# A spectral network with fused head and dilation: PSUM as single and triple tiles, and a new order of bursts, sums and head steps

## The chip, the cores and the metric

The kernel runs on one core of a Trainium2 chip. The metric is device time in microseconds (us), the median of repeated runs of the whole program. The engines are TensorE (PE in the profile; PEld is its weight load), VectorE (DVE), ScalarE (ACT), GpSimd (POOL) and SyncE (SP, which here only starts transfers). TensorE writes its results to PSUM, an on-chip memory of eight banks; a bank has 512 float32 columns on 128 partitions. VectorE and ScalarE read the banks and write to SBUF, the large on-chip memory. All arithmetic is float32, and one float32 matmul appears in the trace as two instructions ("x32" for 16 matmuls).

## The reference

The input is 8 images of 8 channels and 256 x 256 pixels. Channels fall into 4 groups.

```python
def net(x):                                   # x: group-normalised image
    h = conv1x1(concat(x, gridx, gridy))      # fc0, 4 groups x 10 channels
    for i in range(4):
        f = rfft2(h)                          # only 24 x 12 coefficients are used
        f = einsum('bgixy,gioxy->bgoxy', f, w[i])
        h = irfft2(f) + conv1x1(h, w_w[i], w_b[i])
        if i < 3: h = swish(h, beta[i])
    h = swish(conv1x1(h, fc1), beta[3])       # 4 groups x 128 hidden
    return conv1x1(h, fc2)                    # 2 channels a group

x = x + net(group_norm(x))
x = x + dilation3x3(group_norm(x))            # maximum of 9 shifted copies
```

## The kernel before

**Stages of an image.** The spectra are truncated, so each transform is a small matrix product. `spectrum_x` (L231) normalises the image and forms the first layer's spectrum; `spectrum_h` (L326) does so for layers 1 to 3 from rows that were summed while the layer before ran. `mix` (L361) multiplies the spectrum with the weights on VectorE, and TensorE folds the result. `rows_of` (L406) turns it into `zt`, the coefficients of every row, in five rounds of two outputs each, with one two-bank PSUM tile a round (matmuls L413, or L417 in odd layers; copies L195). Then `layer` (L432) goes over the image in 11 chunks, taken in 6 pairs (the last pair has one chunk).

**What a layer does with a chunk.** The four pieces are functions within `layer`.

- `burst(c)` fills four banks: 16 matmuls for the 1x1 convolution (L488; L485 in layer 0), then 8 that add the inverse transform from `zt` (L491). ScalarE empties the banks with two activations (SiLU at L497; in layer 3 an addition of a bias at L499, and the chunk is stored to DRAM).
- `turn(c)`: VectorE transposes the chunk in 32 x 32 blocks, in two halves (L439), into one of three parts of the buffer `turned`.
- `transform(k)` is the row transform of pair k, which the next layer's spectrum needs: 32 matmuls into four banks (L456), and two copies of 960 columns back into `turned` (L201 on VectorE, L199 on ScalarE).
- `gather(k)` sums the result over the blocks with a constant matrix (4 matmuls into one bank, L470), and VectorE copies it into `zt` (L473, or L476 for pairs whose chunks lie the other way round).

**The head of the image before.** Between these pieces run the 128 steps of the previous image's fc1 and fc2. `first(n)` is fc1 for 512 pixels a group: 4 matmuls into four banks (L635) and two SiLU activations of 1024 columns (L637). `second(n)` is fc2 for two steps together: 8 matmuls into one bank (L657), which VectorE adds to the residual (L662; L660 for the first of each eight). A step n that is even does `second(n - 4)` and then `first(n)`; an odd one does only `first(n)`. So an even step has 12 matmuls, an odd one 4.

**Who sets the order.** The order on TensorE, VectorE and ScalarE is the program's. A layer is a generator; each `yield (1,)` in it runs one head step and after it one operation of the dilation of an earlier image (`dilate`, L686 to L722: maxima at L704, L706, L709 with L710, and a normalising and adding part to L720). The strings "even" and "odd" make one extra step if the count of steps has the other parity, so that the even steps fall where the layer wants them. Numbers that are yielded outside the layers (spectrum, mix, rows) are shares of a step; there the head fills the gaps. Layers 0 to 2 take 11 steps each, layer 3 takes two for each chunk. Image 0 has no head beside it, and the last image's head runs alone at the end.

```python
        for k in range((NCH + 1) // 2):
            c = 2 * k
            burst(c)
            if k > 1: gather(k - 2)
            yield (1,)          # even head step: second, first
            turn(c)
            burst(c + 1)
            if k > 0: transform(k - 1)
            yield (1,)          # odd head step: first
            turn(c + 1)
```

**PSUM.** All tiles have one tag, "z": two banks each, four buffers, used in turn. A burst, a transform and a first take two of these tiles, a rows_of round takes one, and everything that needs one bank (`ps_a`: gather, second, the sums of the normalisation) takes a whole tile of two and uses half of it. A tile is reused as soon as its reader has finished, so with four buffers a group of four banks can be filled while the group before it is emptied.

Of the kernel before, what the change touches and what calls it, by code (L numbers as in the profile page):

```python
# [19 lines left out]
HW = 256  # L20
# [24 lines left out]
def fno_dilate_kernel(ctx: ExitStack, tc: tile.TileContext, a: dict, out: bass.AP):  # L45
# [10 lines left out]
    def ps_z(name):  # L56
        return ps.tile([128, 2, 512], F32, tag="z", bufs=4, name=name)

    def ps_a(name):
        return ps_z(name)[:, 0, :]  # L60
# [91 lines left out]
    p = ps_z("p_wc")  # L152
# [43 lines left out]

    def copy_2(i, dst, src):
        if i % 2:
            nc.scalar.activation(dst, src, AF.Identity)  # L199
        else:  # L200
            nc.vector.tensor_copy(dst, src)  # L201

# [28 lines left out]
    def spectrum_x(b, out_):  # L231
# [22 lines left out]
        for half in range(2):  # L254
            xn = x[:, half].rearrange("p (r w) -> p r w", r=8)
            for r in range(0, 8, 4):
                t = ps_z(f"p_xt_{b}_{half}_{r}")
                for i in range(8):
                    nc.tensor.transpose(
                        t[:, i // 4, 128 * (i % 4) : 128 * (i % 4 + 1)],  # L260
                        xn[:, r + i // 2, 128 * (i % 2) : 128 * (i % 2 + 1)], ident,
                    )
                dst = xt[half][:, :, r : r + 4, :].rearrange("p f (u r) c -> p u r f c", u=2)
                src = t.rearrange("p u (r f c) -> p u r f c", r=2, f=2)
                for u in range(2):
                    copy(u, dst[:, u], src[:, u])
                yield 1.4
# [138 lines left out]
    def rows_of(b, l):  # L406

        zv = zt[:, :, :, : NBLK * WID].rearrange("p r f (n o) -> p o n r f", n=NBLK)
        for o in range(0, WID, 2):
            p = ps_z(f"p_g_{b}_{l}_{o}")  # L410
            for u in range(2):
                if l % 2 == 0:
                    mm(p[:, u, : NBLK * CS * NQ], fz[:, o + u].rearrange("p g k -> p (g k)"),  # L413
                       rowg.rearrange("p n j r -> p (n j r)"), start=True, stop=True)
                else:
                    for g in range(G):
                        for j in range(NQ):  # L417
                            mm(p[part(j), u, NBLK * CS * g : NBLK * CS * (g + 1)], fz[:, o + u, g, :],
                               rowg[:, :, j, :], start=True, stop=True)
            for u in range(2):  # L420
                src = p[:, u, : NBLK * CS * NQ]
                if l % 2 == 0:
                    dst = zv[:, o + u].rearrange("p n r f -> p n f r")
                    src = src.rearrange("p (n f r) -> p n f r", n=NBLK, r=CS)
                else:
                    dst = zv[:, o + u].rearrange("p n r f -> p f n r")
                    src = src.rearrange("p (f n r) -> p f n r", f=NQ, n=NBLK)
                copy(u, dst, src)
            yield 0.7


    def layer(b, l, out_, stored, side):  # L432
        group_in_f = l % 2 == 1

        def turn(c):

            dst = turned[:, c % 3].rearrange("p (s f x) -> p f s x", s=2, f=NQ)
            for i in range(2):
                nc.vector.transpose(  # L439
                    dst[:, 2 * i : 2 * i + 2], h[:, c, 2 * i : 2 * i + 2].rearrange("p f (s x) -> p f s x", s=2))  # L440
# [5 lines left out]
        def transform(k):  # L446
# [6 lines left out]
            pair = [ps_z(f"p_d_{b}_{l}_{k}_{i}") for i in range(2)]  # L453
            for v in range(8):
                for q in range(NQ):
                    mm(pair[q // 2][part(v % 4), q % 2, : 240 * n], fw8[part(q), v, :],  # L456
                       t[part(q), :, :, v, : NBLK * WID], start=v < 4, stop=v >= 4)
            e = turned[:, (2 * k + 1) % 3, : 960 * n].rearrange("p (q x) -> p q x", q=NQ)
            for i in range(2):
                copy_2(i, e[:, 2 * i : 2 * i + 2], pair[i][:, :, : 240 * n])  # L460

        def gather(k):
# [5 lines left out]
            for g in range(NQ):  # L468
                m = e[:, :, :, g] if group_in_f else e[:, g].rearrange("p q r i -> p r q i")
# [8 lines left out]
        def burst(c):  # L478
            pair = [ps_z(f"p_z_{b}_{l}_{c}_{i}") for i in range(2)]
            for f in range(NQ):  # L480
                for q in range(NQ):
                    o = pair[q // 2][part(f), q % 2, :]
# [6 lines left out]
            for s in range(2):  # L489
                for q in range(NQ):  # L490
                    mm(pair[q // 2][:, q % 2, HW * s : HW * (s + 1)],  # L491
                       zt[part(q), 2 * c + s].rearrange("p f o -> p (f o)"), binv[part(q), :],
                       start=False, stop=s == 1)
            for i in range(2):
                dst = h[:, c, 2 * i : 2 * i + 2, :]
                if l < 3:
                    nc.scalar.activation(dst, pair[i], AF.Silu)  # L497
                else:
                    nc.scalar.activation(dst, pair[i], AF.Identity, bias=bias3)  # L499
# [8 lines left out]
        if l == 0:  # L508
# [3 lines left out]
            nc.vector.tensor_scalar(wcn, wc, out_["mr"][:, 1:2], None, ALU.mult)  # L512
        if l == 3:

            yield "odd"
# [6 lines left out]
        yield "even"  # L522
        for k in range((NCH + 1) // 2):
# [5 lines left out]
            turn(c)  # L529
            if c + 1 < NCH:  # L530
                burst(c + 1)
            if k > 0:
                transform(k - 1)
# [81 lines left out]
    def head(b, stored, stats):  # L615
# [13 lines left out]
        def first(n):  # L629
# [3 lines left out]
            pair = [ps_z(f"p_fc1_{b}_{n}_{i}") for i in range(2)]  # L633
            for g in range(G):
                mm(pair[g // 2][:, g % 2, :], w1[part(g), blk, :], hs[k][part(g), :], start=True, stop=True)  # L635
            for i in range(2):
                nc.scalar.activation(act[:, 2 * i : 2 * i + 2, :], pair[i], AF.Silu)  # L637
# [37 lines left out]
        for n in range(STEPS):  # L675
            if n % 32 % NBLK == 0:
                load_state(n // 32 * NCH + n % 32 // NBLK + 2)
            if n % 2 == 0 and n > 3:
                second(n - 4)
            first(n)  # L680
            yield
        second(STEPS - 4)
# [248 lines left out]
```

## Time and profile before

| | |
|---|---|
| time, median of 3 runs | 3992.06 us (3990.4 to 3992.45) |
| span of the profiled execution | 4004.3 us |
| ScalarE busy | 2812.6 us, 70% |
| period of an image with a head beside it (layer 3's first burst to the next one's) | about 477.6 us |
| of it layer 3 and the next image's spectrum, to layer 0's first burst | 106.1 us (1707.78 to 1813.93) |
| layers 0 to 2, first burst to last gather | 74.1 us in layer 0, about 70 in the others |
| between the layers: last gather to the next layer's first burst | 50.4 us (1888.01 to 1938.46) |
| head of the last image alone | about 3690 to 3974 us |

The lines of the profile are read so: in a timeline, a line is a group of instructions of one engine: when it began (us), how long it took in all, the engine, the source line, the operation, the tile written and the tiles read, the tile shape of a matmul (contracted rows * output rows) and its operand's size (partitions x columns), and the number of instructions; in brackets how long the engine stood idle before it, and whose instruction ended that. A matmul group's length in the trace includes its draining, so consecutive groups overlap a little; the distance from one start to the next tells better what a group costs.

### The profile page before, as it was taken

What the parts mean: (1) busy time and instruction counts of PE and PEld (TensorE: products, weight loads), DVE (VectorE), ACT (ScalarE), POOL (GpSimd) and SP (SyncE); (2) the same over time, 40 slices, a digit from 0 to 9 for tenths busy, and PEclk for the clock granted to TensorE, in tenths of its full rate; (3) what the DMA queues carried; (4) which work ended last, traced back from release to release, by engine and by line L of the source; (5) the groups of instructions that cost most, each with busy time, mean ns of one, the idle gap of its engine ahead of it and who ended that gap; (6) DMA issues with size and microseconds to landing.
All of it is one profiled execution on the core that took longest, in us unless ns stands there. A gap on an engine that the chain in (4) does not pass through costs nothing. (4 is left out here: it accounts for less than half of the span.)

```text
span 4004.3 us, 118649 instructions
## 1 busy us (share of the span) xinstructions
PE 3743.3 (93%) x53530; PEld 1450.1 (36%) x53530; DVE 2567.1 (64%) x3679; ACT 2812.6 (70%) x2945; POOL 117.1 (3%) x202
## 2 busy tenths in 40 slices
PE   5767999999999999999999999999999999999997
PEld 3333333333333333333333333333333333333221
DVE  6765666557776666766766676766776666673533
ACT  2435777767777777777777777777777777778886
POOL 1000000000000000000000000000000000000000
PEclk7888999999999999999999999999999999999998
DMA  3005111431225222251123511244111522115311
GB/s 85 15 16 190 51 35 42 151 111 59 61 68 178 80 59 59 88 190 54 59 59 106 184 50 50 59 149 134 59 59 50 185 87 67 59 51 196 99 49 47
DMA packets 113985, 345.05 MB, mean 86 GB/s; under 512 B 15768, under 2 KB 18392, under 8 KB 98056
## 3 DMA queue, kind: packets, MB, share of 16 engines
q1 hardware_dynamic: 95288, 276.33, 22.0%
q0 software_dynamic: 18192, 61.13, 4.7%
q8 instruction: 421, 6.90, 0.7%
q14 instruction: 84, 0.69, 0.1%
HBM read 213.40 MB, written 123.74 MB: 84 GB/s over the span
## 5 line engine op out<-in xcount | busy, mean ns | idle before, releaser
L637 ACT ACTIVATE act<-p_fc 128x1024 f32<-128x1024 f32 x2048 | 1961.2, 1026 | 754.6 <-PE p_fc L635 753.6
L635 PE MATMUL p_fc<-hs,c_w 32*128 32x512 f32 x8192 | 1179.6, 631 | 2.7 <-DVE h L660 1.3
L657 PE MATMUL p_fc<-act,c_w 128*32 128x512 f32 x8192 | 1000.7, 602 | 55.0 <-ACT act L637 43.4
L439 DVE STREAM_TRANSPOSE turned<-h 128x1024 f32<-128x1024 f32 x528 | 622.8, 1218 | 17.5 <-ACT h L497 17.4
L635 PEld LDWEIGHTS p_fc<-hs,c_w 32*128 32x128 f32 x8192 | 386.5, 183 | 682.8 <-ACT act L637 296.0
L497 ACT ACTIVATE h<-p_z 128x1024 f32<-128x1024 f32 x528 | 511.9, 1021 | 133.6 <-PE p_z L491 133.1
L662 DVE TENSOR_TENSOR y<-p_fc,y 128x512 f32<-128x512 f32 x392 | 270.7, 691 | 450.4 <-PE p_fc L657 449.3
L657 PEld LDWEIGHTS p_fc<-act,c_w 128*32 128x32 f32 x8192 | 233.0, 110 | 667.4 <-issue 403.7
L491 PE MATMUL p_z<-c_binv,zt 32*128 32x256 f32 x5632 | 417.3, 411 | 0.6 <-ACT zt L193 0.6
L491 PEld LDWEIGHTS p_z<-c_binv,zt 32*128 32x128 f32 x5632 | 262.6, 189 | 310.1 <-issue 298.1
L488 PE MATMUL p_z<-h,c_wt 32*32 32x512 f32 x8448 | 351.1, 602 | 9.9 <-DVE y L662 7.9
L456 PE MATMUL p_d<-turned,c_fw 32*32 32x480 f32 (+1 forms) x9216 | 306.8, 544 | 1.3 <-DVE turned L439 1.3
L201 DVE COPY turned<-p_d 128x960 f32<-128x960 f32 x144 | 154.6, 1073 | 168.5 <-PE p_d L456 168.5
L195 DVE COPY zt<-p_g 128x264 f32<-128x264 f32 x300 | 160.1, 628 | 146.5 <-PE p_g L413 79.0
L499 ACT ACTIVATE h<-p_z,c_bias 128x1024 f32<-128x1024 f32 x176 | 186.6, 1111 | 44.0 <-PE p_z L491 43.7
L371 DVE TENSOR_REDUCE S<-turned 128x80 f32<-128x800 f32 x192 | 188.8, 983 | 5.2
L368 DVE TENSOR_TENSOR turned<-t,B 128x800 f32<-128x800 f32 x192 | 188.4, 981 | 0.6 <-DMA t<-in_spw 0.3
L332 DVE STREAM_TRANSPOSE turned<-zt 128x960 f32<-128x960 f32 x96 | 175.1, 1858 | 0.6
L456 PEld LDWEIGHTS p_d<-turned,c_fw 32*32 32x32 f32 x9216 | 121.6, 103 | 143.1 <-issue 80.6
L199 ACT ACTIVATE turned<-p_d 128x960 f32<-128x960 f32 x144 | 130.3, 905 | 58.7 <-PE p_d L456 58.7
L488 PEld LDWEIGHTS p_z<-h,c_wt 32*32 32x32 f32 x8448 | 84.3, 103 | 227.6 <-issue 72.6
L470 PE MATMUL p_u<-turned,c_stack 128*32 128x480 f32 (+1 forms) x1152 | 136.5, 545 | 15.2 <-DVE turned L201 13.1
(171 smaller groups left out, 1955.4 us busy)
## 6 DMA issues: line engine op xcount, KB each, us to landing
stored<-h SPq DMA_DIRECT2D x88, 1024.0 KB
hs<-stored SPq DMA_DIRECT2D x352, 256.0 KB
t<-in_spw SPq DMA_DIRECT2D x96, 400.0 KB
yin<-y_rows POOLq DMA_DIRECT2D x56, 512.0 KB, 5.0
h<-in_xp SPq DMA_DIRECT2D x352, 48.0 KB
turned<-in_x SPq DMA_DIRECT2D x16, 1024.0 KB
y<-in_x SPq DMA_DIRECT2D x56, 256.0 KB
y_rows<-y POOLq DMA_DIRECT2D x56, 256.0 KB, 2.3
```

What stands on the lines that cost most here:

```text
L368: nc.vector.tensor_tensor(pr, sw[k], bt[:, k2, k].unsqueeze(2).to_broadcast([128, G, 2 * WID, WID]), ALU.mult)
L371: nc.vector.tensor_reduce(s[k2][:, k].rearrange("p g s o -> p (g s o)"), pr.rearrange("p g m i -> p (g m) i"), AX.X, ALU.add,)
L439: nc.vector.transpose(dst[:, 2 * i : 2 * i + 2], h[:, c, 2 * i : 2 * i + 2].rearrange("p f (s x) -> p f s x", s=2))
L456: mm(pair[q // 2][part(v % 4), q % 2, : 240 * n], fw8[part(q), v, :], t[part(q), :, :, v, : NBLK * WID], start=v < 4, stop=v >= 4)
L488: mm(o, wt[part(q), l, g, :], h[part(q), c, f, :], start=True, stop=False)
L491: mm(pair[q // 2][:, q % 2, HW * s : HW * (s + 1)], zt[part(q), 2 * c + s].rearrange("p f o -> p (f o)"), binv[part(q), :], start=False, s ...
L497: nc.scalar.activation(dst, pair[i], AF.Silu)
L499: nc.scalar.activation(dst, pair[i], AF.Identity, bias=bias3)
L635: mm(pair[g // 2][:, g % 2, :], w1[part(g), blk, :], hs[k][part(g), :], start=True, stop=True)
L637: nc.scalar.activation(act[:, 2 * i : 2 * i + 2, :], pair[i], AF.Silu)
L657: mm(acc[part(g), :], w2[:, g, 15 - rb - i : 47 - rb - i], act[:, g, :], start=i == 0, stop=i == 1)
L662: nc.vector.tensor_tensor(y, sums, y, ALU.add)
```

## The change

**PSUM.** The eight banks are now two single-bank tiles (tag "one") and two tiles of three banks (tag "tri"). A group of four banks is a single and a triple. Gather, second and the small sums take a single, so they no longer hold a bank that they don't use. ScalarE's activations work on 512 and 1536 columns instead of 1024 twice; in the transform VectorE copies 480 columns and ScalarE 1440.

**Order in a pair.** The even chunk's burst, the sum (gather) of the pair two before, and a head step; then the first half of the even chunk's turn, the transform of the pair before, and the turn's other half; then the odd chunk's burst, and the other head step. Before, the transform came after the odd burst. It is meant to bring groups with the same matmul tile shape together.

**Head steps.** A step does `first(n)` ahead of `second`, and `second(n - 3)` belongs to odd steps. TensorE thus sees first, first, second, where it saw second, first, first. Layer 3 begins with an even step.

**Sum's columns.** Gather reads its columns in the order (row, block, column) that its copy expects in all layers; before, they came in another order in both layer parities. `rows_of` works in rounds of 4, 4 and 2 outputs.

```diff
-    def ps_z(name):
-        return ps.tile([128, 2, 512], F32, tag="z", bufs=4, name=name)
     def ps_a(name):
-        return ps_z(name)[:, 0, :]
+        return ps.tile([128, 512], F32, tag="one", bufs=2, name=name)
+    def ps_tri(name):
+        return ps.tile([128, 3, 512], F32, tag="tri", bufs=2, name=name)
+    def ps_four(name):
+        one, tri = ps_a(f"{name}_0"), ps_tri(f"{name}_1")
+        return one, tri, [one] + [tri[:, i, :] for i in range(3)]
...
         # transform
-            for i in range(2):
-                copy_2(i, e[:, 2 * i : 2 * i + 2], pair[i][:, :, : 240 * n])
+            nc.vector.tensor_copy(e[:, 0], one[:, : 240 * n])
+            nc.scalar.activation(e[:, 1:4], tri[:, :, : 240 * n], AF.Identity)
...
         # gather
-                m = e[:, :, :, g] if group_in_f else e[:, g].rearrange("p q r i -> p r q i")
+                m = e[:, :, :, g].rearrange("p q r i -> p r q i") if group_in_f else e[:, g]
...
         # burst
-            for i in range(2):
-                dst = h[:, c, 2 * i : 2 * i + 2, :]
+            for dst, src in ((h[:, c, 0, :], one), (h[:, c, 1:4, :], tri)):
...
+        yield "even"
         if l == 3:
-            yield "odd"
...
-        yield "even"
         for k in range((NCH + 1) // 2):
             c = 2 * k
             burst(c)
             if k > 1:
                 gather(k - 2)
             yield (1,)
-            turn(c)
+            turn(c, (0,))
+            if k > 0:
+                transform(k - 1)
+            turn(c, (1,))
             if c + 1 < NCH:
                 burst(c + 1)
-            if k > 0:
-                transform(k - 1)
             yield (1,)
...
         # head
-            for i in range(2):
-                nc.scalar.activation(act[:, 2 * i : 2 * i + 2, :], pair[i], AF.Silu)
+            nc.scalar.activation(act[:, 0, :], one, AF.Silu)
+            nc.scalar.activation(act[:, 1:4, :], tri, AF.Silu)
...
-            if n % 2 == 0 and n > 3:
-                second(n - 4)
             first(n)
+            if n % 2 and n > 2:
+                second(n - 3)
             yield
-        second(STEPS - 4)
         second(STEPS - 2)
```

In the changed file the lines are: first L633 with its activations L634 and L635, second L655 with its adds L658 and L660, burst L488 and L491 with L496 and L498, transform L456 with its copies L459 (VectorE) and L460 (ScalarE), gather L470 with L473 and L476, dilation L701 to L717.

## The prediction

> **What bounds the kernel now.** I read the page's busy times and costliest groups first, then the timeline of TensorE in each stage, then the other engines' timelines in the same windows.
>
> From the page:
>
> ```profile
> PE 3743.3 (93%) x53530; PEld 1450.1 (36%) x53530; DVE 2567.1 (64%) x3679; ACT 2812.6 (70%) x2945; POOL 117.1 (3%) x202
> ```
>
> TensorE is occupied nearly always; ScalarE and VectorE mostly wait for it. So what counts is how long TensorE takes for its list, in order, with every wait in it. One pair of chunks, with its two head steps, is this on TensorE (start, duration, line):
>
> ```profile
> 1958.99 1.33 PE L488 MATMUL p_z<-h,c_wt 32*32 32x512 f32 x32
> 1960.25 1.15 PE L491 MATMUL p_z<-c_binv,zt 32*128 32x256 f32 x16
> 1961.33 1.01 PE L470 MATMUL p_u<-turned,c_stack 128*32 128x480 f32 x8
> 1962.15 1.90 PE L657 MATMUL p_fc<-act,c_w 128*32 128x512 f32 x16
> 1963.98 1.14 PE L635 MATMUL p_fc<-hs,c_w 32*128 32x512 f32 x8
> 1965.06 1.18 PE L488 MATMUL p_z<-h,c_wt 32*32 32x512 f32 x32
> 1966.17 1.15 PE L491 MATMUL p_z<-c_binv,zt 32*128 32x256 f32 x16
> 1967.24 2.24 PE L456 MATMUL p_d<-turned,c_fw 32*32 32x480 f32 x64
> 1969.41 1.14 PE L635 MATMUL p_fc<-hs,c_w 32*128 32x512 f32 x8
> 1970.55 0.62 PE L488 MATMUL p_z<-h,c_wt 32*32 32x512 f32 x2
> ```
>
> Start to start is what a group costs: even burst 1.26 + 1.08, gather 0.82, second 1.83, first 1.08, odd burst 1.11 + 1.07, transform 2.17, first 1.14; the pair is 11.56. Only about 0.2 of it is waiting (1.26 against 1.11, 1.14 against 1.08). VectorE in the same pair:
>
> ```profile
> 1962.40 0.66 DVE L473 COPY zt<-p_u 128x480 f32<-128x480 f32 x1 [1.00 <-PE p_u L470]
> 1964.12 0.69 DVE L662 TENSOR_TENSOR y<-p_fc,y 128x512 f32<-128x512 f32 x1 [1.06 <-PE p_fc L657]
> 1964.73 2.36 DVE L439 STREAM_TRANSPOSE turned<-h 128x1024 f32<-128x1024 f32 x2
> ```
>
> Each waits for TensorE and none is waited for: the turn of the odd chunk is over 2 us before the gather's copy, and the transform comes last. In layer 3 a chunk and its two steps take 6.40 us:
>
> ```profile
> 2191.90 1.14 PE L488 MATMUL p_z<-h,c_wt 32*32 32x512 f32 x32
> 2192.97 1.16 PE L491 MATMUL p_z<-c_binv,zt 32*128 32x256 f32 x16
> 2193.93 1.20 PE L635 MATMUL p_fc<-hs,c_w 32*128 32x512 f32 x8
> 2195.32 1.92 PE L657 MATMUL p_fc<-act,c_w 128*32 128x512 f32 x16 [0.19 <-ACT h L499]
> 2197.17 1.19 PE L635 MATMUL p_fc<-hs,c_w 32*128 32x512 f32 x8
> 2198.29 0.71 PE L488 MATMUL p_z<-h,c_wt 32*32 32x512 f32 x16
> ```
>
> The 1.9 us of L657 lie between the two L635, and so cover ScalarE's emptying of the burst, which the next L635 needs:
>
> ```profile
> 2194.15 2.12 ACT L499 ACTIVATE h<-p_z,c_bias 128x1024 f32<-128x1024 f32 x2 [0.20 <-PE p_z L491]
> ```
>
> Where heads run alone, two steps take 4.17 us, 0.3 of it a wait for ScalarE:
>
> ```profile
> 3800.73 1.92 PE L657 MATMUL p_fc<-act,c_w 128*32 128x512 f32 x16 [0.30 <-ACT act L637]
> 3802.58 2.03 PE L635 MATMUL p_fc<-hs,c_w 32*128 32x512 f32 x16
> 3804.89 1.92 PE L657 MATMUL p_fc<-act,c_w 128*32 128x512 f32 x16 [0.28 <-ACT act L637]
> ```
>
> **What the Trainium skill says.** "PSUM — Partial Sum Buffer", section "Engine vs sequencer instructions": matmuls start and complete in program order. So one that waits for a bank holds up everything behind it; the trace agrees (L657 above, 0.30 late, delays L635). "TensorEngine Tiling (Array Packing)", section "Key Properties": a change of tiling mode drains TensorE. The trace agrees, and it is cheap: L635 to L657 (mode changes) starts 0.52 after the last matmul began, against 0.43 between groups of one mode. "ScalarE: Activation LUTs", section "What ACT_TABLE_LOAD costs": 186 ns + 0.833 ns an element. The trace has 1026 ns for 1024 and 972 and 571 ns for L199's 960 and 480 elements, so 171 + 0.835 an element, which I use. "Perfetto Trace Analysis", section "Matmuls": groups should rotate through banks so that emptying one overlaps the next. That is the question here: whether two single and two triple tiles still do.
>
> **The change part by part.**
>
> *Sizes.* Activations over 512 and 1536 columns take 0.60 and 1.45 us and start 0.5 and 1.34 apart: with overlap 1.96 for both, as the two of 1024 (1.94). The transform's copies go from 960 + 960 to 480 on VectorE (0.66 instead of 1.16) and 1440 on ScalarE (1.37 instead of 0.97): ScalarE's pair goes from 4 x 1.94 + 0.97 = 8.7 to 9.1 us of over 11, so it is hidden. The sum's new column order reads the same 480 columns in another order: the same four matmuls, cost nothing. Both layer parities take 0.83 there today.
>
> *Order in a pair.* New list on TensorE: even burst, gather, first, transform, odd burst, first, second. With the starts above, and transform followed by odd burst in one mode (image 0: 91.54 to 94.77, 3.23 for both up to L491): 1.11 + 1.08 + 0.95 (gather, now a mode change behind it) + 1.07 + 3.23 + 0.97 (L491 to L635, no change of mode) + 0.97 + 1.85 = 11.22, if nothing waits. The new wait is the transform's. It needs the odd chunk's turn, and as its single tile is the gather's, also L473's copy. Both stand on VectorE behind the add for second, which is now the last thing of the pair before. From the even burst's start: add from 0.14, 0.61 to the next start, then a dilation operation (0, or 1.13 for L704 or L706, or about 1.33 for L709 with L710, in turn), turn 2.29, copy 0.66, semaphore 0.06: 3.99, 4.9 or 5.1 (without a dilation operation the copy begins at 3.27, after the gather). TensorE is there at 4.21, and ScalarE has emptied the even burst at 4.33. So the transform starts at 4.33, 4.92, 5.12, mean 4.79, and the pair is 4.79 + 7.02 = 11.81: +0.25. Pair 0 has no gather and no transform, so its odd burst waits for the even burst's triple tile, free at 4.33: 4.33 + 4.90 = 9.2 against 8.6 without its first wait: +0.6. Pair 1 +0.1, pair 5 +0.24. Per layer 0.6 + 0.1 + 3 x 0.25 + 0.24 = 1.7; 21 layers run beside heads: **+35**.
>
> *Image 0* has no heads to fill in: odd burst, activation to 2.08, turn to 4.50, transform at 4.56 after the next even burst begins; then 3.23 + 1.08 = 8.87 against 7.63 (99.17 - 91.54). 4 pairs x 3 layers x 1.24: **+15**.
>
> *Layer 3.* New list: burst, first, first, second. Two triple tiles: the second first needs the burst's. L491 starts at 1.11 and is done 1.15 later; activations with the bias from 2.31, ended 2.10 later, at 4.41; so that first starts its triple part at 4.47, where TensorE is ready at 3.0. Then 0.98 and second 1.85: 7.31 against 6.40, +0.91. Of image 1 to 6's eleven chunks four are bare and two half so (in others the next image's spectrum fills the gap): 4.6 each, 28; image 7's eleven are all bare, 10: **+38**.
>
> *Heads alone.* first, first, second: second now waits for the 0.60 single activation, not 1.03, so that wait goes. But each second first needs the triple of its predecessor, the last thing ScalarE does: with ScalarE's 3.8 us a cycle both conditions meet at 3.94, not 4.17. Last image, some 55 cycles: **-12**.
>
> *Between layers* the same 0.23 is gained in about 6 cycles (1.4), but L473's follower, the four turns of zt and p_b, is VectorE's (add, then the last turn of 1.86, p_b stalls 1.8 where it stalled up to 1.3), and rows_of empties three banks at once, so the first behind it waits 1.0 and p_g 0.9. I take **0**, bounds -1.2 and +1.5 a stage, x21.
>
> Sum: 35 + 15 + 38 - 12 = +76; 3992 + 76 = **4068**.
>
> **Rivals.**
> *A, the tiles suffice (faster):* emptying keeps ahead. Pairs 11.22 (5 x 21 x -0.34 = -36), between layers -1.2 (-25), image 0 and layer 3 unchanged, heads -12: 3919. For it: VectorE idles 1 us before each add, ScalarE 30%. Against: they idle at the wrong moments; the waits are chains. Chance 0.09.
> *B, gains and losses cancel:* the between-layer gain is full (-25), the transform's wait half (pairs +0, pair 0 alone: +17 a run instead of 35), image 0 and layer 3 half (+26), heads -12: 3998. Chance 0.08.
> *C, more of it:* rows_of and p_b cost 1.5 a stage (+32): 4100. For it: VectorE's order there is unfavourable. Chance 0.18.
> *Forecast:* 0.65.
>
> **How the numbers follow.** The forecast's own bounds are the dilation wait (0.1 to 0.9 in a pair, +-15) and the bare chunks (+-10). Range 4000 to 4115, from B to past C; A lies outside. Faster 0.10 (A and a little of B), same 0.05 (B), slower 0.85 (the rest).
>
> **What would show it.** Pairs of 11.4 to 12.1 us with TensorE waiting at L456 for VectorE's L473; layer 3's bare chunk at 7.3, waiting at the second L633 for L498; image 0's pairs at 8.9; heads alone under 4.17. If bare chunks stay at 6.4 or pairs fall to 11.2, the ring of two is deep enough and I am wrong.

## The result, and the profile after

The changed kernel takes 4145.51 us (median; 4137.67 to 4146.07). The runs of before on the same chip have a median of 3992.26 us, so it is 153 us slower; the ratio of the means is 1.0379, with a 95% interval of 1.0365 to 1.0394. The forecast was slower, 4068 us, with 4115 as the upper end of the range; the loss is twice the forecast.

From the page of after (third part of a group's line: the idle time ahead of it, and what ended it):

```profile
PE 3733.2 (90%) x53530; PEld 1462.3 (35%) x53530; DVE 2500.9 (60%) x3679; ACT 2848.7 (69%) x2945; POOL 117.4 (3%) x202
L660 DVE TENSOR_TENSOR y<-p_fc,y 128x512 f32<-128x512 f32 x392 | 270.4, 690 | 780.2 <-PE p_fc L655 780.1
L456 PE MATMUL p_d<-turned,c_fw 32*32 32x480 f32 (+1 forms) x9216 | 309.6, 541 | 80.2 <-DVE turned L439 42.0
```

TensorE does the same 53530 matmul instructions in 10 us less of busy time, VectorE is busy for 66 us less, ScalarE for 36 us more at 69%. The trace is 140 us longer, and TensorE stands idle in it for 150 us more. Two waits stand here: TensorE ahead of the transform, 80 us (1.3 before), and VectorE ahead of its add for fc2, 780 us (450 before).

To find where, I cut both traces at the starts of TensorE's groups: each layer from its first burst to its last gather, the stretch between that and the next layer's first burst, layer 3's first ten chunks, and what follows until the next image's first burst. Some head steps now fall into a neighbouring stretch, so I took 1.07 us for each first and 1.83 us for each second off the stretch that has more. In us:

| stretch | before | after, against before | predicted |
|---|---|---|---|
| image 0 (no head beside it) | 317.2 | +19.7 | +15 |
| layers 0 to 2, images 1 to 7 | 1510.7 | +0.1 | +35 |
| between the layers, images 1 to 7 | 1092.0 | +37.8 | 0 |
| layer 3, first ten chunks, images 1 to 7 | 532.3 | +50.1 | +38 for all eleven |
| last chunk of layer 3, and mix and rows_of of the next image | 162.6 | +42.7 | no term of its own |
| the end: last chunk of image 7 and the head alone | 302.6 | -11.8 | -12 |

With 1.1 us ahead of the first burst the sum is the 139.8 us of the two spans (4144.1 and 4004.3). The traced execution of before, at 4004.3 us, was 12 us longer than the median time, so 13 of the 153 us stand in no row.

**The granted clock is part of it.** Behind layer 3 TensorE's clock is at half for 41.0 us in the trace of after, in images 1 to 5, and never in that of before. In layer 0 of images 1 to 7 it is the other way round: 44.4 us at half clock before, 20.5 after. Here is image 4's stretch at half clock (in a view by windows: busy time of PE, PEld, DVE, ACT and POOL with the number of instructions, then the granted share of the clock, 0.50, and the DMA), then p_f, the matmuls that fold the mix's result, in it, in image 6 at full clock, and in the trace of before:

```profile
2364.40:2374.60 10.20, 8.86 (x54) 5.07 (x58) 4.44 (x13) 1.94 (x2) 0.00 (x0) 0.50 0.09 22
2365.01 1.82 PE L384 MATMUL p_f<-F,c_fold 32*32 32x120 f32 x32 [3.14 <-DVE F L376]
3362.36 1.02 PE L384 MATMUL p_f<-F,c_fold 32*32 32x120 f32 x32 [3.14 <-DVE F L376]
1795.31 1.02 PE L387 MATMUL p_f<-F,c_fold 32*32 32x120 f32 x32 [1.09 <-ACT act L637]
```

The stretch behind layer 3 takes 30.99 us in image 6, whose clock stays full, and 31.85 to 34.31 us in images 1 to 5; these differences add up to 12.9 of the 42.7 us. A pair that holds one half-clock window of 3.4 us takes about 1.6 us more (13.91 against 12.28 us in layer 0 of e3 below), so the 23.9 us fewer at half clock in layer 0 are worth about 11 us, an estimate from these figures: at equal clock the layers would show about +12 and not +0.1. The half-clock windows behind layer 3 go with the wait ahead of these matmuls. In the runs where it is 2.0 us or more, 46 of 54 images have one; in those where it is 1.24 us or less, none of 36. No run tests whether the wait is the cause.

A pair in layer 2 of after, from its timeline (TensorE's and VectorE's lines that the prediction spoke of):

```profile
2185.62 0.69 DVE L660 TENSOR_TENSOR y<-p_fc,y 128x512 f32<-128x512 f32 x1 [3.07 <-PE p_fc L655]
2187.55 2.36 DVE L439 STREAM_TRANSPOSE turned<-h 128x1024 f32<-128x1024 f32 x2
2189.84 0.62 DVE L473 COPY zt<-p_u 128x480 f32<-128x480 f32 x1
2190.51 2.19 PE L456 MATMUL p_d<-turned,c_fw 32*32 32x480 f32 x61 [0.78 <-DVE zt L473]
```

This is the chain that was forecast: add, dilation operation, turn, copy, transform. The transform starts 5.03 us after the even burst (2185.48); 4.33, 4.92 or 5.12 were worked out. The pairs from the third on take 11.24, 12.00 and 12.05 us in images 2 to 7, 11.76 in the mean, where 11.81 was forecast and 11.56 is the time before. Image 1, which has no dilation operations beside it, has 11.24 us in all three.

A bare chunk of layer 3 of after, the same view:

```profile
1771.20 1.16 PE L488 MATMUL p_z<-h,c_wt 32*32 32x512 f32 x32
1773.25 2.06 PE L633 MATMUL p_fc<-hs,c_w 32*128 32x512 f32 x10
1773.45 2.12 ACT L498 ACTIVATE h<-p_z,c_bias 128x512 f32<-128x512 f32 x2 [1.61 <-PE p_z L491]
1775.62 1.13 PE L633 MATMUL p_fc<-hs,c_w 32*128 32x512 f32 x6 [0.31 <-ACT h L498]
1778.54 1.05 PE L488 MATMUL p_z<-h,c_wt 32*32 32x512 f32 x18
```

It takes 7.34 us (1778.54 - 1771.20). L633's matmuls stop after ten instructions and go on when L498 ends: the second first waits for ScalarE to empty the burst.

### The profile page after: what moved, and what is told of

It is laid out like the page before. It is cut to its first block, busy times and chain, and to the rows that moved or that the text cites. A ratio compares the mean times of both kernels' runs of the same rounds, so it can differ in the third digit from the quotient of the medians.

```text
span 4144.1 us, 118033 instructions
## 1 busy us (share of the span) xinstructions
PE 3733.2 (90%) x53530; PEld 1462.3 (35%) x53530; DVE 2500.9 (60%) x3679; ACT 2848.7 (69%) x2945; POOL 117.4 (3%) x202
## 4 chain that ended last, share of the span: by engine, by line
PE 71%; DVE 16%; ACT 6%; issue 5%; DMA 1%; POOL 0%; DVEq 0%; SPq 0%; POOLq 0%; ACTq 0%
PE p_fc L655 21%; PE p_fc L633 19%; PE p_z L491 7%; PE p_d L456 7%; PE p_z L488 6%; DVE turned L439 4%; ACT h L498 3%; DVE turned L329 3%; PE p_b L338 2%; PE p_g L412 2%; PE p_z L485 2%; DVE y L660 2%; ACT h L496 2%; PE p_g L417 2%; PE p_u L470 1%
## 5 line engine op out<-in xcount | busy, mean ns | idle before, releaser
L635 ACT ACTIVATE act<-p_fc 128x1536 f32<-128x1536 f32 x1024 | 1492.4, 1457 | 13.0 <-PE p_fc L633 12.3
L633 PE MATMUL p_fc<-hs,c_w 32*128 32x512 f32 x8192 | 1223.9, 631 | 64.0 <-ACT h L498 15.4
L655 PE MATMUL p_fc<-act,c_w 128*32 128x512 f32 x8192 | 989.2, 601 | 16.5 <-ACT act L634 9.3
L634 ACT ACTIVATE act<-p_fc 128x512 f32<-128x512 f32 x1024 | 614.9, 600 | 490.4 <-PE p_fc L633 476.8
L660 DVE TENSOR_TENSOR y<-p_fc,y 128x512 f32<-128x512 f32 x392 | 270.4, 690 | 780.2 <-PE p_fc L655 780.1
L439 DVE STREAM_TRANSPOSE turned<-h 128x1024 f32<-128x1024 f32 x528 | 636.5, 1227 | 115.2 <-ACT h L496 114.9
L496 ACT ACTIVATE h<-p_z 128x512 f32<-128x512 f32 (+1 forms) x528 | 511.9, 1021 | 264.8 <-PE p_z L491 263.2
L633 PEld LDWEIGHTS p_fc<-hs,c_w 32*128 32x128 f32 x8192 | 395.9, 185 | 634.5 <-ACT act L634 162.7
L655 PEld LDWEIGHTS p_fc<-act,c_w 128*32 128x32 f32 x8192 | 216.1, 109 | 720.5 <-issue 387.6
L491 PE MATMUL p_z<-c_binv,zt 32*128 32x256 f32 x5632 | 404.8, 401 | 0.0
L456 PE MATMUL p_d<-turned,c_fw 32*32 32x480 f32 (+1 forms) x9216 | 309.6, 541 | 80.2 <-DVE turned L439 42.0
L488 PE MATMUL p_z<-h,c_wt 32*32 32x512 f32 x8448 | 359.0, 599 | 5.3 <-ACT h L496 2.5
L491 PEld LDWEIGHTS p_z<-c_binv,zt 32*128 32x128 f32 x5632 | 255.4, 184 | 302.5 <-issue 292.6
L460 ACT ACTIVATE turned<-p_d 128x1440 f32<-128x1440 f32 x144 | 183.1, 1272 | 164.5 <-PE p_d L456 164.5
L498 ACT ACTIVATE h<-p_z,c_bias 128x512 f32<-128x512 f32 (+1 forms) x176 | 186.6, 1111 | 159.1 <-PE p_z L491 158.7
L199 DVE COPY zt<-p_g 128x264 f32<-128x264 f32 x300 | 163.9, 612 | 93.9 <-PE p_g L412 40.3
L456 PEld LDWEIGHTS p_d<-turned,c_fw 32*32 32x32 f32 x9216 | 125.2, 103 | 261.2 <-ACT h L496 67.7
L488 PEld LDWEIGHTS p_z<-h,c_wt 32*32 32x32 f32 x8448 | 94.8, 103 | 203.5 <-ACT act L634 98.1
L470 PE MATMUL p_u<-turned,c_stack 128*32 128x480 f32 (+1 forms) x1152 | 138.2, 543 | 4.9 <-ACT turned L460 2.5
```

The costliest lines, as they stand in the source:

```text
L439: nc.vector.transpose(dst[:, 2 * i : 2 * i + 2], h[:, c, 2 * i : 2 * i + 2].rearrange("p f (s x) -> p f s x", s=2))
L456: mm(banks[q][part(v % 4), : 240 * n], fw8[part(q), v, :], t[part(q), :, :, v, : NBLK * WID], start=v < 4, stop=v >= 4)
L488: mm(o, wt[part(q), l, g, :], h[part(q), c, f, :], start=True, stop=False)
L491: mm(banks[q][:, HW * s : HW * (s + 1)], zt[part(q), 2 * c + s].rearrange("p f o -> p (f o)"), binv[part(q), :], start=False, stop=s == 1)
L496: nc.scalar.activation(dst, src, AF.Silu)
L498: nc.scalar.activation(dst, src, AF.Identity, bias=bias3)
```

## The experiments

The parts are called P (PSUM tiles, with rows_of and the copies that go with them), O (order in a pair) and H (order of head steps and the even start of layer 3). The fourth part, the sum's columns, was not run alone: in layers with heads a gather that is followed by a first takes 0.943 us from its start to the next one's in the changed kernel, and 0.942 to 0.946 in the runs below that have the old column order. By this measure it costs and brings nothing on TensorE.

Where each run differs from before, in the stretches of the table above (us, corrected in the same way), and its time:

| run | image 0 | layers 0-2 | between | layer 3 | behind it | end | time |
|---|---|---|---|---|---|---|---|
| changed kernel | +20 | 0 | +38 | +50 | +43 | -12 | 4145.5 |
| e1: P | +1 | -4 | +21 | +18 | +6 | -10 | 4042.8 |
| e2: H | -2 | +43 | +32 | +25 | +41 | +1 | 4143.0 |
| e3: O | +3 | +84 | +1 | -4 | 0 | -1 | 4088.9 |
| e4: P, O | +25 | +74 | +22 | +12 | +6 | -7 | 4137.5 |
| e5: P, H | 0 | +22 | +38 | +50 | +41 | -9 | 4147.6 |
| e6: H, O | +1 | +40 | +30 | +25 | +39 | +4 | 4144.9 |
| e7: changed, fc2 ahead of fc1 | +22 | -27 | +19 | +12 | +37 | -6 | 4065.7 |
| e8: O, fc2 ahead of fc1 | 0 | +7 | -2 | -6 | +22 | -1 | 4037.2 |
| e9: H, add late | -2 | +108 | +18 | +61 | +14 | -1 | 4213.5 |
| e10: even start alone | -3 | -11 | +1 | +25 | +25 | -1 | 4038.6 |
| e11: changed, rows of two | +20 | -8 | +53 | +52 | +43 | -10 | 4167.7 |
| e12: P, rows of two, copies | +6 | +129 | +58 | +16 | +21 | -5 | 4231.1 |
| e13: changed, odd start | +20 | -4 | +39 | +15 | +14 | -9 | 4084.1 |
| e14: H, odd start | -3 | +47 | +28 | +10 | +17 | +2 | 4105.2 |
| e15: H, add late between layers | -2 | +49 | +25 | +23 | +42 | -2 | 4133.2 |

No run is faster than before. e1, e8 and e10 lie less than 2% above it and e7 about there, but no interval reaches 1. The rows add up to 3 to 29 us less than the differences in time, since the traced execution of before was a long one; the gap is largest for e8, e9 and e11, whose traced executions were 11 to 12 us below their medians.

Two columns above all hold clock as well as order. In layer 0 of images 1 to 7 TensorE was at half clock for 44.4 us before, 20.5 in the changed kernel and in e10, 17.1 in e1, 3.4 in e7, but 88.7 in e3 and e12 and 92.2 in e4. At the price above, about 21 us of e3's 84 are clock, and so are the -11 of e10 and most of e7's -27. Behind layer 3 it was 34 to 41 us in the changed kernel, e2, e5, e6, e7 and e15, 20.5 in e8 and e10, 10 in e11, 7 in e9 and e14, and none in the others. In layers 1 and 2 it was at full clock in every run.

### One part or two of the change (e1 to e6)

**e1: P alone**, the PSUM hunks of the diff on the kernel before.

```diff
-        return ps.tile([128, 2, 512], F32, tag="z", bufs=4, name=name)
+        return ps.tile([128, 512], F32, tag="one", bufs=2, name=name)
+        return ps.tile([128, 3, 512], F32, tag="tri", bufs=2, name=name)
```

> The kernel before with only the PSUM tiles of the change (two single banks, two triples, and rows_of in rounds of 4, 4 and 2); order of head steps and of the pair as before. Theory T (the prediction's: two triple tiles are too few, and the second fc1 of a layer 3 chunk waits for the burst's triple): most of the loss is here, 4090 us or more, bare chunks of layer 3 at about 7.3 us. Theory H (the head order costs it: fc2 after both fc1 leaves nothing to cover the emptying of a burst, and puts the add, with all that VectorE has behind it, at the end of a step): 3980 to 4010 us, bare chunks of layer 3 at 6.4 us, since fc2 still stands between the two fc1.

4042.79 us, ratio 1.0126 (1.0111 to 1.0141): between the two theories. Bare chunks of layer 3 take 6.12 us, less than the 6.40 of before, so theory T, which was the prediction's, has the wrong cause for them. What P costs is elsewhere: pairs take 11.78 us (the triple of the transform is free only when ScalarE has copied 1440 columns; TensorE's weight load for the even burst waits 0.33 us for it), which with the gains of other pairs makes 8 us in layers 1 and 2, the stretch behind layer 1 costs 20 us in seven images, and the chunks of layer 3 that share with the next image's spectrum grow.

**e2: H alone.**

```diff
-            yield "odd"
+            yield "even"
...
-            if n % 2 == 0 and n > 3:
-                second(n - 4)
             first(n)
+            if n % 2 and n > 2:
+                second(n - 3)
```

> The kernel before with only the new head order (fc1, fc1, fc2; layer 3 begins with an even step); four PSUM tiles of two banks as before. Theory T: within 20 us of before, bare chunks of layer 3 at about 6.4 us. Theory H: slower by 100 us or more, bare chunks of layer 3 at about 7.3 us also with double tiles, and TensorE waits longer for VectorE at p_f (L387 before) and p_b (L341) than the 73 and 27 us of before.

4142.98 us, ratio 1.0381 (1.0364 to 1.0398): as slow as the whole change. Bare chunks take 7.35 us with four double tiles. TensorE waits 72 us for VectorE at p_f (the fold of the mix) and 41 us at p_b (the spectrum's matmuls behind the turns of zt), where it waited 48 and 19 before; with its other waits there it is 88 and 49, against the 73 and 27 that the expectation names. Theory H has this run right.

**e3: O alone.**

```diff
-            turn(c)
+            turn(c, (0,))
+            if k > 0:
+                transform(k - 1)
+            turn(c, (1,))
             if c + 1 < NCH:
                 burst(c + 1)
-            if k > 0:
-                transform(k - 1)
```

> The kernel before with only the new order in a pair (transform between the halves of the even chunk's turn, ahead of the odd burst). Here the even step still does fc2 and then fc1, between gather and transform, so the turn of the odd chunk has 2.9 us more until the transform needs it. Theory H: no new wait, fewer changes of tile shape, a pair of about 11.25 instead of 11.56 us, in all 20 to 35 us faster than before (about 3962), with image 0 slower by some 15 us of it (about 3975 in all). Theory T says nothing of the sort: with the transform's wait for the turn of the odd chunk, as the prediction had it, pairs of 11.8 us and 15 to 35 us slower.

4088.9 us, ratio 1.0246 (1.0228 to 1.0264): slower, against theory H. Theory T had the direction, but not the wait. The timeline of the end of a pair, TensorE and ScalarE:

```profile
2145.03 1.04 PE L634 MATMUL p_fc<-hs,c_w 32*128 32x512 f32 x8
2145.24 1.94 ACT L496 ACTIVATE h<-p_z 128x1024 f32<-128x1024 f32 x2 [1.16 <-PE p_z L490]
2146.32 1.05 PE L487 MATMUL p_z<-h,c_wt 32*32 32x512 f32 x4 [0.25 <-ACT h L496]
```

The odd burst, a first and the next even burst now follow each other. The even burst needs the odd burst's banks, and ScalarE takes 1.94 us to empty them, of which the first covers 1.04. Pairs take 12.28 us. Before, the transform stood between the two bursts. The transform itself waits little, 7 us in the whole run: that chain needs the new head order.

**e4 to e6: two parts at a time.**

> The whole change but for the head order and the sum's column order, which are as before. Theory T: about as slow as the whole change, 4100 us or more. Theory H: no slower than before, 3960 to 4000 us: the head order is what costs the 150 us.

> The whole change but for the order in a pair and the sum's column order. Theory W (a group of four banks takes ScalarE about 2 us to empty and its banks are asked for again after one other group of four; a wait arises where only one fc1 of 1.1 us stands between, so the parts' costs overlap or cancel and don't add): the pairs are not helped by the new pair order, so the layers beside heads cost 40 to 60 us more than before, the stages outside them 100 to 130, image 0 nothing: 4140 to 4180 us. Theory S (the costs of the parts simply add): 51 + 151, about 4194 us.

> Both new orders, with the PSUM tiles (four of two banks) and the sum's column order as before. Theory W: the two orders cancel within the layers (there the transform then stands where the head order leaves a gap), what stays is the head order's loss outside the layers, about 100 us, and image 0 as in the run with the pair order alone (+3): 4085 to 4115 us. Theory S: 151 + 97, about 4240 us.

P with O: 4137.5 us, 1.0365 (1.0345 to 1.0386), theory T's number, though H is not in it; theory H had 3960 to 4000 us. P with H: 4147.61 us, 1.0384 (1.0361 to 1.0406), as theory W had it in all, but the layers cost 22 us and not 40 to 60. H with O: 4144.9 us, 1.0387 (1.0372 to 1.0403), against theory W: with double tiles the two orders don't cancel in the layers (+40; pairs of 11.74, 12.29 and 12.34). Theory S, that the parts add, is wrong for P with H (202 us, measured 158) and for H with O (248, measured 156), and for the whole change, which would take 4291 us (51 + 151 + 97). P with O does fit the sum, 148 us against 145.5, but not stretch by stretch: image 0 costs 25 us and not 4. H sets what is lost behind layer 3, and about half of layer 3 and most of the loss between the layers. P adds to layer 3. In layers 1 and 2, where no clock differs, H costs 39 us, O 42, both together 43, and the whole change 13.

Image 0 is much slower only where P and O meet (e4, e7, e11, e13, the changed kernel). There a pair takes 8.87 us, with O alone 7.89. The views show why. With O alone the odd chunk's turn begins when the first activation of 1024 columns is done, 1.05 us after ScalarE began (170.38 after 169.33); in the changed kernel it begins after both, 1.97 us after ScalarE began (177.04 after 175.07), since the turn's first half reads columns 0 to 1023 and the activations now cover 0 to 511 and 512 to 2047. That is 0.92 of the 0.98 us between the pairs.

### fc2 between the two fc1 again (e7, e8)

```diff
-            first(n)
             if n % 2 and n > 2:
                 second(n - 3)
+            first(n)
```

> The changed kernel with one swap: in an odd head step fc2 (second) comes ahead of fc1 (first), so that TensorE sees fc1, fc2, fc1 instead of fc1, fc1, fc2; nothing else is altered. Theory W: fc2's 1.85 us again stand between a burst's emptying and the next fc1 in layer 3 (bare chunks 6.1 to 6.4 us instead of 7.34), the add comes earlier on VectorE; what stays is image 0 (+22) and the losses of the PSUM tiles outside the layers (about 36): 4020 to 4055 us. Theory S: PSUM and pair order cost 145 together as measured, so about 4135 us.

> The kernel before with the new pair order, the sum's column order and the head order fc1, fc2, fc1 of the run above; PSUM tiles as before. Theory W: no two groups of four banks with only one fc1 between them in the pairs, no new wait, and the transform beside the burst saves changes of tile shape: pairs about 11.25 us, everything else as before: 3955 to 3985 us, faster than before. Theory S: the pair order's cost stays, 4080 us or more.

e7: 4065.73 us, ratio 1.0187 (1.0172 to 1.0202): 80 us of the loss come back by swapping two lines; theory W had 4055 us at most. Bare chunks take 6.1 us, pairs 11.48 instead of 11.76. e8: 4037.2 us, 1.0112 (1.009 to 1.0134), not the gain that was expected: its pairs are 11.66, slightly over the 11.56 of before, because the even first takes 1.29 instead of 1.07 us, and 22 us go behind layer 3, in part with 20.5 us at half clock.

### The add at the end of a step (e9, e15)

VectorE's order between the layers, two lines from the timeline of before, then those of after with the matmul that waits:

```profile
2141.26 3.68 DVE L332 STREAM_TRANSPOSE turned<-zt 128x960 f32<-128x960 f32 x2
2144.85 0.67 DVE L662 TENSOR_TENSOR y<-p_fc,y 128x512 f32<-128x512 f32 x1
2223.18 0.69 DVE L660 TENSOR_TENSOR y<-p_fc,y 128x512 f32<-128x512 f32 x1 [1.34 <-PE p_fc L655]
2223.79 1.80 DVE L329 STREAM_TRANSPOSE turned<-zt 128x960 f32<-128x960 f32 x1
2225.74 0.52 PE L338 MATMUL p_b<-turned,c_eh_f 128*32 128x120 f32 x10 [1.55 <-DVE turned L329]
```

The last turn of zt needs nothing from fc2. Before, the last two turns run ahead of the add; now the last one is queued behind an add that idles 1.34 us for fc2, and p_b waits 1.55 us for the turn. e9 takes H alone and issues the add one head step later.

```diff
+            flush()             # the add of the step before
             first(n)
             if n % 2 and n > 2:
                 second(n - 3)
```

> The run with the head order alone, but VectorE's add for fc2 is issued one head step later, so that what VectorE does for the next stage is not queued behind an fc2 that TensorE has only just begun; the matmuls' order is the same. Theory A (the loss between the layers is VectorE's queue: the add stands behind an fc2 at the end of its step, the turns of zt and the spectrum's products stand behind the add, and p_b and p_f wait for them): about 60 us less than the 4143 us of that run, 4070 to 4100, the waits at p_f and p_b back near 73 and 27 us; bare chunks of layer 3 stay at 7.35 us, since ScalarE sets these. Theory C (it is only that the steps fall otherwise in these stages since layer 3 begins with an even step): 4130 to 4155 us.

4213.54 us, ratio 1.0554 (1.0522 to 1.0586): in all a miss for both theories. But the waits went where theory A said. TensorE's waits in e2:

```profile
PE p_f L386 <- DVE F L378: 72.1, 17, 13.0
PE p_b L340 <- DVE turned L331: 40.9, 22, 7.5
```

and in e9 (us in total, times, the longest):

```profile
PE p_f L386 <- DVE F L378: 46.7, 4, 13.4
PE p_b L340 <- DVE turned L331: 14.9, 2, 7.5
```

Between and behind the layers e9 loses 31 us where e2 loses 73; behind layer 3 the wait of 3.14 us at p_f is gone, and with it most of the half clock (41.0 us in e2, 6.8 in e9). In the layers and in layer 3 the late add costs 101 us more (pairs of 12.63 us); the cause of that is open. e15 has the late add in the steps between the layers alone:

> The run with the head order alone, with VectorE's add one step later only in the stages between the layers (steps within layers as in that run). Theory A: the 44 us that these stages gave back in the run with every add late come, without the cost within the layers: 4090 to 4110 us. If the gain there was only moved from the layers: 4130 us or more.

4133.21 us, 1.035 (1.0334 to 1.0367), a miss for theory A. The stretch ahead of layer 3 gives back 12 us, the one behind layer 3 nothing (+42). There the last two steps belong to layer 3 and are not late in this run; that this is the reason is argued only.

### The start of layer 3 (e10, e13, e14)

```diff
         if l == 3:
-            yield "odd"
+            yield "even"
```

> The kernel before with one word altered: layer 3 begins with an even step, the order within steps as before (fc2, fc1, then fc1), so the list of a bare chunk is burst, fc2, fc1, fc1. Theory C (the shifted steps cost the time between the layers): 4040 us or more. Theory A and W (fc2 is well placed, right behind the burst, and the add is not last in its step): 3985 to 4015 us, bare chunks at 6.4 to 6.6 us.

e10, the kernel before with that word altered, 4038.61 us, 1.0113 (1.0097 to 1.0128), near theory C's number, with a bare chunk of 7.23 us that neither theory had. Its list is burst, fc2, fc1, fc1. The timeline of TensorE and ScalarE at the end of a chunk:

```profile
2203.75 2.01 PE L635 MATMUL p_fc<-hs,c_w 32*128 32x512 f32 x16
2204.99 1.94 ACT L637 ACTIVATE act<-p_fc 128x1024 f32<-128x1024 f32 x2 [0.87 <-PE p_fc L635]
2206.06 0.62 PE L488 MATMUL p_z<-h,c_wt 32*32 32x512 f32 x2 [0.30 <-ACT act L637]
```

fc2 covers the burst well, and now the next burst waits, for the first of the two fc1. Burst, fc1, fc1, fc2 waits at the second fc1; burst, fc2, fc1, fc1 waits at the burst. In the bare chunk the two fc1 in succession are what costs, whether fc2 stands ahead of them or behind.

e13 and e14 set that word back to "odd", in the changed kernel and in H alone, so that a bare chunk is burst, fc1, fc2, fc1.

> The changed kernel with one word set back: layer 3 begins with an odd head step again, so a bare chunk is burst, fc1, fc2, fc1 though the order within the steps is the new one. Theory F (two fc1 in succession is what layer 3 pays for, wherever fc2 stands, and the shifted start costs the stage behind it): bare chunks at 6.1 to 6.4 us, layer 3 and the stage behind it some 50 to 75 us less: 4070 to 4095 us. If it is the new order within the step itself: 4125 us or more.

> The run with the head order alone (4143 us), but layer 3 begins with an odd step as before: with it before, the even start alone and both, four runs of two edits. Theory F: bare chunks at 6.4 us; what stays is the pairs (12.1 us) and the add behind the last fc2 of a step between the layers: 4075 to 4105 us. If the two edits' costs merely add: 4143 - 46 = 4097 us as well, but then bare chunks stay above 6.8 us.

e13: 4084.08 us, ratio 1.0225 (1.0208 to 1.0242). One word is 61 us of the 153. Bare chunks, from the timeline of TensorE:

```profile
2235.24 1.15 PE L488 MATMUL p_z<-h,c_wt 32*32 32x512 f32 x32
2238.27 1.92 PE L655 MATMUL p_fc<-act,c_w 128*32 128x512 f32 x16
2241.21 1.37 PE L488 MATMUL p_z<-h,c_wt 32*32 32x512 f32 x26
```

5.97 us here and 6.24 for the next; there is no wait in brackets here, nor at the fc1 on either side of fc2. Layer 3 falls from +50 to +15, what lies behind it from +43 to +14, about 13 us of that with the half clock, of which nothing is left there. e14: 4105.17 us, 1.0278 (1.0257 to 1.03), bare chunks mostly at 6.4 to 6.7 us. e13 is as theory F had it, e14 at the edge of its range, and both keep the new order within the steps.

### rows_of and the copies (e11, e12)

```diff
-        for o0 in range(0, WID, 4):      # rounds of 4, 4, 2 in single and triple
+        for o in range(0, WID, 2):       # rounds of 2, in two banks of a triple
```

> The changed kernel with rows_of in rounds of two outputs (two banks of a triple) as before, all else as changed. Theory B (rounds of four banks are what costs the time between the layers): 20 to 40 us less, 4105 to 4125 us. Theory A: within 10 us of the changed kernel, 4135 to 4155 us.

4167.67 us, 1.0431 (1.0414 to 1.0447): 22 us slower than the changed kernel. Theory B has the wrong direction, and theory A expected no difference. These rounds use the two triples alone, with a bank of each left empty, so rounds of two in tiles of their own remain untested.

e12 takes P alone with these rounds, and shares the transform's copies out evenly again.

```diff
-            nc.scalar.activation(e[:, 1:4], tri[:, :, : 240 * n], AF.Identity)
+            nc.vector.tensor_copy(e[:, 1], tri[:, 0, : 240 * n])
+            nc.scalar.activation(e[:, 2:4], tri[:, 1:3, : 240 * n], AF.Identity)
```

> The kernel before with the PSUM tiles of the change, rows_of in rounds of two, and the transform's copies divided evenly again (VectorE the single and one bank of the triple, ScalarE two banks), so that the triple comes free earlier. If the run with the PSUM tiles alone lost its time to rows_of after layer 1 (+20) and to the transform's 1440-column copy (pairs 11.78 instead of 11.56), while it gained in bare chunks (6.12 us instead of 6.40) and at the end (-10): 3975 to 4010 us. If the two triples are too few in general: 4035 us or more.

4231.11 us, 1.0595 (1.0577 to 1.0613): the worst of all, and no test of what it was made for. ScalarE's copy, from the timeline:

```profile
2217.93 0.97 ACT L458 ACTIVATE turned<-p_d 128x960 f32<-128x960 f32 x1 [1.57 <-DVE turned L457]
```

It reads two banks of the triple and waits 1.57 us for VectorE, which reads the third: the two engines no longer copy at the same time, as they do in e1. The profile puts the wait down to a semaphore, so the program sets it; that the banks themselves would force it is not shown. Pairs take 12.69 us.

## Why the prediction was right and wrong

**Right: the direction, and three steps with their causes.** The pair (11.81 us forecast, 11.76 measured), with the chain that makes it; image 0's pair (8.87 forecast, 8.87 measured); heads alone (-12 forecast, -11.8 measured; the cycle's median is 3.98 us, forecast 3.94).

**Wrong: "Between layers ... I take 0".** This is the step that failed. The prediction named the waits (the add ahead of the last turn of zt, p_b) and bounded them at +1.5 us a stage. Measured are 37.8 us in 21 stages, 1.8 each and so beyond the bound, and unevenly: 0.3 us behind layer 0, 1.8 behind layer 1, 3.3 behind layer 2, where the last turn waits for the add. The 13 us behind layer 1 are not settled: e7 removes them, a late add doesn't, and P alone has 20 us there.

**What follows layer 3's last chunk was in no term,** and costs 42.7 us in six images. Of these 5.6 are the last chunks' own 0.94. VectorE's products for the next image queue behind the same adds, so the wait at p_f grows from 1.09 to 3.14 us, 12.3 us in all. Only one fc1 now stands between p_f and p_g (the matmuls of rows_of), and p_g waits 1.61 us for VectorE where it didn't before, about 10 us. The half clock takes 12.9. That leaves 2. e9 shows the add's share: with the add out of the way p_f doesn't wait. e10 and e13 show the other one: the even start alone makes p_f wait 3.12 us, and with the odd start the changed kernel's wait falls to 1.24 us. These two shares overlap, and how much is which can't be separated. The prediction priced every stretch at one clock; that the clock could fall behind a longer wait was not in it.

**Too small: layer 3.** +38 was forecast for eleven chunks, measured are 50.1 + 5.6. Four bare chunks were counted in images 1 to 6, but there are five, with the last one. The chunks that share with the next image's spectrum were counted at less than they cost: the fifth to eighth at nothing, where they take 40.3 us in image 2 against 37.6. P alone shows that these are a cost of their own: its bare chunks are faster than before, and its layer 3 is 18 us slower.

**Right number, wrong cause: the bare chunk and pair 0.** The bare chunk (7.31 forecast, 7.34 measured) was put down to two triple tiles in place of four double ones. H alone has it with double tiles (7.35), P alone hasn't (6.12). The wait comes from two fc1 in succession, which either set of tiles has too few banks for. Pair 0 (+0.6 forecast; 9.11 against 8.55 us in layer 2) was put down to the triple tile as well, but H alone has 9.44 us and P alone 8.23. There too the head order leaves a single fc1 between two bursts. That both numbers fit is luck.

**Too large: the layers.** +35 was worked out for a layer as in layer 2 of images 2 to 7, and taken times 21. Layer 2 does cost 11.1 us in seven images (1.6 each). But image 1's pairs, with no dilation operation, are shorter than before (11.24 against 11.56), layer 1 costs only 2.3 us, and layer 0 gains 13.2, most of it because less of it ran at half clock in this trace. That these 35 us too many nearly balance the 37.8 missing between the layers is luck; without it the forecast would have been further off.

**Image 0:** +15 was forecast, 19.7 measured. In layer 2, at full clock, the cost is 7.4 us and not four pairs of 1.24: the second pair grows by 2.9 us (6.01 to 8.94). In layer 1 it grows by 4.3 (to 10.34), with 3.4 us at half clock in it. Layer 0 shows only +0.4, since 13.7 us of its first two pairs ran at half clock before and none after. Layer 3 has 3.6 more.

Rivals A and B, in which the gains carry or cancel the losses, are out. C had the right stretch and too little of it. A's pair of 11.22 us does occur, as 11.24, but only where no dilation operation lies in the chain: in image 1, and in one of the three pairs in images 2 to 7.

## What to carry to other kernels

With eight banks and groups of four, as in this kernel, a group's banks are asked for again after one other group. Write down what lies between for every group in the order, and compare it with what ScalarE needs (here 2 us): two short groups in succession cost the difference, 0.9 us here, and it doesn't help to have a long one before or after them. An operation that waits for a long group at the end of a step should not stand ahead of work that waits for nothing; ask for each stretch of the kernel, not only for the inner loop, what is queued behind it. Moving that operation is no sure cure: issued later everywhere, the add cost 71 us more (e9 against e2). Parts of a change that each cost alone may cancel or add, stretch by stretch, so run them alone and together before naming one. And before a difference between two traces is put down to the order, compare the granted clock of the same stretch in both.

## What had not been expected

- Two engines that read different banks of one PSUM tile took turns, by a wait in the program: ScalarE waited 1.57 us for VectorE (e12), while with a tile for each engine the copies start together (2118.84 us for both in e1).
- A split of the banks as 1 and 3 undoes the fit with work that is split in halves: in image 0 the turn began 1.97 us after its activations did, not 1.05 (the changed kernel against O alone).
- A shift of the head steps by one, with everything else the same, costs 46 us (e10).
- TensorE's clock fell to half for up to 10.2 us at a time behind layer 3 in images 1 to 5 of the changed kernel and not in image 6, although the wait at p_f was 3.14 us in all six.
